# Moving the last down products of a conditioned FFN beside attention, with its mixing, zero fill, lists and loads

## The chip, the cores and the metric

The kernel runs on one core of one Trainium2 chip. The metric is the device time of one execution in microseconds, the median over several runs. The engines are written as in the profile: PE (matrix products), PEld (loading of PE's weights, which overlaps), DVE (vector), ACT (activations), POOL, SP (which here only issues transfers). ACT and POOL issue transfers too. DMA stands for the 16 transfer engines.

## The reference, cut to what matters

Everything is float32. `x` has 4 batches of 512 tokens and 256 columns; `cond` gives eight weights for each batch.

```python
def reference(x, cond, ...):
    # 1. conditioned FFN: each batch uses the expert of its largest condition
    e = argmax(cond, -1)
    c = (silu(x @ Wu[e].T + bu[e]) * (x @ Wg[e].T + bg[e])) @ Wd[e].T + bd[e]
    # 2. attention over 512 tokens: 16 query heads of 16 columns, one shared k and v
    x = x + softmax(q(c) @ k(c).T) @ v(c) @ Wo.T + bo
    # 3. a dense layer whose weights are mixed from 8 for each batch
    w = einsum('bg,got->bot', cond, weight * mask)
    t = x @ w[b].T + bias2
    # 4. top-2 routing over 8 experts, 128 places for each expert in each group
    #    of 256 tokens, then gelu(t @ wi[e]) @ wo[e], weighted and summed
    return x + moe(t)
```

## The kernel before

The tile program is written out by hand: the order in which the Python code emits the instructions is the order on each engine. Five stretches follow each other on PE.

*The conditioned FFN* (`hidden`, L268; `down`, L258). For each of four batches `b`, `hidden(b, hc)` makes a quarter of the hidden columns: products with two weights into two PSUM banks (L279, L281), Silu on ACT (L283), a product on DVE (L284) into the tile `hid`. `down(b, dc)` multiplies `hid` by the second weights, 512 tokens at a time in four accumulated products (L263), and ACT adds the bias and writes `coT` (L264). Batches 0 to 2 are emitted by the loop at L347. Beside it DVE mixes the third part's weights: `mixed(b, g)` (L244) adds expert `g`'s masked weights `w2_sb` into `wb_sb` of batch `b`; there are 32 of them, four emitted after each quarter from (1, 1) on. In batch 2's quarters the first attention's projections are emitted (L359): the queries go through DRAM (`qd`, L319 and L320) to reach the layout of the score products.

*The zero fill* (L361). ACT's queue writes zeros to `xp`, the buffer in DRAM to which tokens are scattered later; 8,712 KB in one transfer.

*The lead* (L797). Attention runs in 64 steps, 16 for each batch. Step `n` makes the exponentials for step `n` and the row maxima for step `n + LEAD`, with `LEAD = 6`. So six sets of maxima are made first (`maxima`, L366: four products of 32 rows, L375, and four reductions on DVE, L379). The list `before_steps` (L789) says what PE does between them: batch 3's hidden quarters, the down products of batches 2 and 3, and, for the third part, `turn_mixed` (L689, transposes of the mixed weights) and `route_mixed` (L700, their product with the router).

*Attention* (L1123). A step has `maxima`, `exponentials` (L396: products L405, Exp on ACT L409) and `weigh` (L414: products L423 with the exponentials of the step before). Four 32-row products use the array together, two of maxima and two of exponentials. Two forms of a step exist. The sparse one weighs in two halves; the dense one puts other PE work (`side`) between its two half sets and weighs once. A step is dense if the table `beside` (or `last`, for batch 3) names PE work at that step. Those tables also hold the later parts of the batches before: values, their normalisation (`inv`, `norm`), output product, `mix` (third part), routing (`choose`, `rank`, `places`, `rows`), and the scatter of the tokens to `xp` on POOL's queue (`send`, `row0` to `row3`; two indirect transfers each, L656).

*The FFN of the experts* (`run`, L1189). Units of 256 or 128 tokens with one expert: fetch weights (`fetch_in`, `fetch_out`: 1 MB each on SP's queue, L912) and rows (`fetch_rows`, L929, which waits for scatters so far), transpose (`turn`, L972, and the DVE copy L980), `up` (L1036, products L1051), `put` (L1077, products L1084) and an adding scatter to the output (L1098). Weight tiles have three buffers each. Which expert and which rows a unit has comes from lists that DVE works out (`list_of_pairs`, L866; `lists_of_rest`, L882). `first_pairs` emits the first ones within the last attention, `place` (L1168) and the table `final` (L761) put batch 3's remaining pieces and the list of the rest between the pieces of the first units.

SBUF is given out by pools: `cp` and `c1p` hold the first part's tiles and are closed at L805, before the attention's pools `ep`, `rp` and `fp` are opened in their place. [...]

Of the kernel before, what the change touches and what calls it, by code (L numbers as in the profile page):

```python
# [42 lines left out]
def adaln_attn_ffn_kernel(  # L43
# [77 lines left out]
    qp = attn_ctx.enter_context(tc.tile_pool(name="qp", bufs=2))  # L121
    c1 = ExitStack()
# [3 lines left out]
    w2_sb = c1p.tile([P, NE, 2 * D], F32, name="w2_sb")  # L126
# [131 lines left out]
    def down(b, dc):  # L258
        w = w_of[b][1]
        wd = w[:, 0:1024].rearrange("p (c d) -> p c d", c=4)  # L260
        po = bank("x")
        for hc in range(4):
            mm(po, wd[:, hc, ts(dc, P)], hid_of[b][:, hc, :], start=hc == 0, stop=hc == 3)  # L263
        nc.scalar.activation(  # L264
            coT[:, dc, ts(b, T)], po, AF.Identity, bias=w[:, 1032 + dc : 1033 + dc]
        )

    def hidden(b, hc):  # L268
        w, w2 = w_of[b]
        wu, wg = (  # L270
            w[:, ds(512 * hc + 256 * n, 256)].rearrange("p (c h) -> p c h", c=2)
            for n in range(2)
        )
        if hc == 0:
            hid_of[b] = cp.tile([P, 4, T], F32, name="hid")
# [71 lines left out]
    for b in range(B - 1):  # L347
        for hc in range(4):
            hidden(b, hc)
            if (b, hc) > (1, 0):  # L350
                for _ in range(4):
                    mixed(*mixing.pop(0))
# [7 lines left out]

    nc.scalar.dma_start(  # L361
        xp.rearrange("(p r) c -> p r c", p=P),
        zeros.unsqueeze(1).to_broadcast([P, NE * EROWS // P + 2, XROW]),
    )

# [334 lines left out]
    def route_mixed(b):  # L700
# [60 lines left out]
    final = {  # L761
# [8 lines left out]

    def side(b, k):

        for off, name in (last if b == B - 1 else beside)[k]:
# [14 lines left out]

    before_steps = [  # L789
        [(hidden, B - 1, 0), (down, B - 2, 0)],  # L790
        [(down, B - 2, 1), (hidden, B - 1, 1), (turn_mixed, 0), (turn_mixed, 1)],
        [(hidden, B - 1, 2), (route_mixed, 0), (route_mixed, 1), (turn_mixed, 2)],
        [(hidden, B - 1, 3), (route_mixed, 2), (turn_mixed, 3)],
        [(down, B - 1, 0), (route_mixed, 3)],
        [(down, B - 1, 1)],
    ]
    for m in range(LEAD):  # L797
        maxima(m, (0, 1, 2, 3))
        if m == 3:
            shifted(0)  # L800
        for f, *of in before_steps[m]:
            f(*of)
        while mixing:
            mixed(*mixing.pop(0))
# [3 lines left out]
    fp = attn_ctx.enter_context(tc.tile_pool(name="fp", bufs=2))  # L808
# [8 lines left out]
    pairs = fp.tile([P, NE + 1], F32, name="pairs", bufs=1)  # L817
    nc.gpsimd.memset(pairs, 0.0)
    texp = fp.tile([P, NUNIT], F32, name="texp", bufs=1)
    table = fp.tile([P, 2, NUNIT], I32, name="table", bufs=1)  # L820
    count = fp.tile([P, 1], I32, name="count", bufs=1)

# [59 lines left out]
    def lists_of_rest():  # L882
        for _ in list_of_pairs(NA, NB):
            pass
        got = fp.tile([P, NE], F32, name="got", bufs=1)
# [17 lines left out]
        nc.vector.tensor_copy(count, most)  # L903
# [43 lines left out]
    def first_pairs(part):  # L947
# [17 lines left out]
        elif part == "5":  # L965
            turn(0, "x")
        else:
            i = fetch_in(2)
            tc.add_manual_dep(i.ins, weighed[-1].ins.name, AFTER, reason="not at once")
            fetch_out(1)  # L970
# [65 lines left out]
    def up(u, half):  # L1036
# [10 lines left out]
        for f0 in range(4 * half, 4 * half + 4, each):  # L1047
            ph = bank("m")
            for k in range(each):
                for c in range(2):  # L1050
                    mm(  # L1051
                        ph[:, ts(k, n)], wi_of[u][:, c, ts(f0 + k, P)], xT_of[u][:, c, :],
                        start=c == 0, stop=c == 1,
                    )
            nc.scalar.activation(  # L1055
# [67 lines left out]
    for n in range(STEPS + 1):  # L1123
        m = n + LEAD
        if n in (0, 27, 43, 56):
# [5 lines left out]
        )  # L1131
# [36 lines left out]
    def place():  # L1168

        for name in final.get(next(places), ()):  # L1170
            if name == "rest":
                lists_of_rest()
                ready.update(range(NA, NUNIT))
                for f, u in late:
                    f(u)
                late.clear()
            else:
                work[B - 1][name]()

    ready, late = set(range(NA)), []  # L1180
# [8 lines left out]
    def run(units, rows, begun=False):  # L1189
# [3 lines left out]
        for k in range(len(units) + 1):  # L1193
            for u in units[k : k + 1]:
                for x in rows(k):
                    fetch_rows(units[x])
                if begun and k == 0:
# [6 lines left out]
                for x in units[k + 3 : k + 4]:  # L1204
                    fetch(fetch_in, x)
# [11 lines left out]
            for x in units[k + 2 : k + 3]:  # L1217
                fetch(fetch_out, x)
# [9 lines left out]
    def rows_behind(k):  # L1228
        return (k + 2,) if k + 2 < len(units) else ()
# [96 lines left out]
```

## Time and profile before

| | |
|---|---|
| median of 3 runs | 650.72 us (650.18 to 651.39) |
| profiled execution | 648.59 us, span 646.9 us |
| mean granted PE clock | 0.992 |
| conditioned FFN up to the first maxima | 0 to 68.2 us |
| lead | 68.2 to 108.8 us |
| first attention, 16 steps | 108.8 to 171.2 us |
| whole attention | 108.8 to 381.9 us |
| FFN of the experts | to 631 us, then the last scatters |

The stretches are read from the timeline of PE: the lead begins with the first product of L375, the first attention with the first of L405. The costliest groups of the page (line, engine, operation, out<-in, tile, count; busy us and mean ns; idle time before them and what ended most of it):

```profile
L379 DVE TENSOR_REDUCE negm<-ps_m 128x1 f32<-128x512 f32 x250 | 160.7, 686 | 63.1 <-PE ps_x L405 43.6
L409 ACT ACTIVATE e<-ps_x 128x512 f32<-128x512 f32 x244 | 132.5, 595 | 100.6 <-PE ps_x L405 96.9
L375 PE MATMUL ps_m<-k,q 32*128 32x512 f32 x500 | 153.3, 639 | 0.0
L405 PE MATMUL ps_x<-q,k 32*128 32x512 f32 x488 | 139.1, 639 | 0.0
L1051 PE MATMUL ps_m<-xT,wi_sb 128*128 128x256 f32 (+1 forms) x672 | 115.5, 330 | 3.2 <-issue 3.2
L1084 PE MATMUL ps_x<-wo_sb,e 128*128 128x256 f32 x512 | 114.3, 379 | 0.0
L423 PE MATMUL ps_a<-e,v 128*32 128x256 f32 (+1 forms) x792 | 75.6, 454 | 0.6 <-ACT e L409 0.2
L263 PE MATMUL ps_x<-hid,wo_sb 128*128 128x512 f32 x64 | 28.8, 597 | 0.0
```

Each product of the program counts twice here, since a float32 product is carried out in two passes. The means are longer than the distance between starts, because the passes overlap; the timeline of PE gives the distance.

### The profile page before, as it was taken

The numbers are of one execution on the slowest core, as the hardware profiler recorded it, in microseconds if no ns is written. First come the engines' busy times: TensorE is split into PE (matmuls) and PEld (weight loads), VectorE is DVE, ScalarE is ACT, GpSimd is POOL, SyncE is SP. The second block draws the span as 40 slices with busy tenths as digits, with TensorE's granted clock in tenths as the row PEclk, the third lists the DMA queues.
The fourth block names the chain that finished last, engine by engine and source line by source line (L and its number), as shares of the span: only waits on it lengthen the run. The fifth ranks groups of instructions, "written<-read, shape, count | busy, mean of one in ns | idle before, by whom it ended". The sixth has DMA issues, their size and how long they took to land.

```text
span 646.9 us, 10162 instructions
## 1 busy us (share of the span) xinstructions
PE 624.3 (97%) x3736; PEld 364.0 (56%) x3736; DVE 335.2 (52%) x831; ACT 226.2 (35%) x404; POOL 111.3 (17%) x146
## 2 busy tenths in 40 slices
PE   8999999999999999999999989999999999999990
PEld 3444454333333433343335268887899999778880
DVE  1174844677768677876887744358222221322320
ACT  1212123566655555654653742221111111111220
POOL 1600000000000000310031141225332222313332
PEclk9999999999999999999999999999999999999996
DMA  7952981300142204321033399736889999888711
GB/s 234 358 167 72 310 269 34 98 19 18 34 132 68 67 18 117 135 68 48 19 121 100 130 334 271 237 99 208 233 275 317 323 333 315 254 275 264 209 20 19
DMA packets 65403, 107.11 MB, mean 166 GB/s; under 512 B 6914, under 2 KB 26946, under 8 KB 65346
## 3 DMA queue, kind: packets, MB, share of 16 engines
q1 hardware_dynamic: 50066, 87.96, 41.8%
q0 software_dynamic: 6400, 8.72, 6.7%
q10 hardware_dynamic: 8880, 9.71, 4.8%
q8 instruction: 31, 0.51, 0.3%
q14 instruction: 26, 0.21, 0.1%
HBM read 79.59 MB, written 26.65 MB: 164 GB/s over the span
## 4 chain that ended last, share of the span: by engine, by line
PE 91%; DMA 2%; DVE 2%; issue 1%; ACT 1%; POOL 1%; SPq 0%; POOLq 0%; DVEq 0%
PE ps_m L375 20%; PE ps_m L1051 17%; PE ps_x L1084 16%; PE ps_a L423 10%; PE ps_a L279 4%; PE ps_x L263 4%; PE ps_x L281 4%; PE ps_x L535 2%; PE ps_x L313 2%; PE ps_x L503 2%; PE ps_x L405 1%; PE ps_a L978 1%; PE ps_x L328 1%; PE ps_x L1018 1%; PE ps_m L995 1%
## 5 line engine op out<-in xcount | busy, mean ns | idle before, releaser
L379 DVE TENSOR_REDUCE negm<-ps_m 128x1 f32<-128x512 f32 x250 | 160.7, 686 | 63.1 <-PE ps_x L405 43.6
L409 ACT ACTIVATE e<-ps_x 128x512 f32<-128x512 f32 x244 | 132.5, 595 | 100.6 <-PE ps_x L405 96.9
L375 PE MATMUL ps_m<-k,q 32*128 32x512 f32 x500 | 153.3, 639 | 0.0
L405 PE MATMUL ps_x<-q,k 32*128 32x512 f32 x488 | 139.1, 639 | 0.0
L1051 PE MATMUL ps_m<-xT,wi_sb 128*128 128x256 f32 (+1 forms) x672 | 115.5, 330 | 3.2 <-issue 3.2
L1084 PE MATMUL ps_x<-wo_sb,e 128*128 128x256 f32 x512 | 114.3, 379 | 0.0
L1051 PEld LDWEIGHTS ps_m<-xT,wi_sb 128*128 128x128 f32 x672 | 103.6, 191 | 13.7 <-issue 4.5
L1084 PEld LDWEIGHTS ps_x<-wo_sb,e 128*128 128x128 f32 x512 | 95.6, 190 | 12.6 <-issue 0.4
L1055 ACT ACTIVATE e<-ps_m 128x512 f32<-128x512 f32 x64 | 38.0, 597 | 173.5 <-PE ps_m L1051 165.7
L375 PEld LDWEIGHTS ps_m<-k,q 32*128 32x128 f32 x500 | 46.5, 183 | 65.7 <-DVE negm L379 36.5
L1098 POOL DMA_INDIRECT out_dram<-y,to_row x36 | 55.5, 1542 | 136.9 <-DVE at L1074 31.6
L423 PE MATMUL ps_a<-e,v 128*32 128x256 f32 (+1 forms) x792 | 75.6, 454 | 0.6 <-ACT e L409 0.2
L423 PEld LDWEIGHTS ps_a<-e,v 128*32 128x32 f32 x792 | 15.6, 108 | 74.9 <-issue 62.5
L980 DVE COPY xT<-ps_a 128x256 f32<-128x256 f32 (+1 forms) x23 | 12.1, 528 | 81.0 <-PE ps_a L978 81.0
L1094 DVE TENSOR_SCALAR y<-ps_x,w 128x256 f32<-128x256 f32 x32 | 15.3, 482 | 58.5 <-PE ps_x L1084 58.5
L656 POOL DMA_INDIRECT xp<-x,to_i x32 | 33.1, 1036 | 55.7 <-DVE negm L379 25.1
L405 PEld LDWEIGHTS ps_x<-q,k 32*128 32x128 f32 x488 | 38.1, 183 | 0.2
L585 POOL TENSOR_SCALAR x<-mk 128x4 f32<-128x4 f32 x4 | 0.8, 211 | 205.4 <-DVE mk L582 205.3
L284 DVE SCALAR_TENSOR_TENSOR hid<-ps_x,wo_sb,sg 128x512 f32<-128x512 f32 x16 | 12.0, 749 | 45.5 <-PE ps_x L281 45.5
L279 PE MATMUL ps_a<-xT_sb,wi_sb 128*128 128x512 f32 x64 | 30.5, 599 | 0.4 <-DMA wi_sb<-in_wcond_dram 0.3
L281 PE MATMUL ps_x<-xT_sb,wi_sb 128*128 128x512 f32 x64 | 30.1, 592 | 0.0
L263 PE MATMUL ps_x<-hid,wo_sb 128*128 128x512 f32 x64 | 28.8, 597 | 0.0
(166 smaller groups left out, 465.1 us busy)
## 6 DMA issues: line engine op xcount, KB each, us to landing
wi_sb<-in_wi_dram SPq DMA_DIRECT2D x25, 1024.0 KB
wo_sb<-in_wo_dram SPq DMA_DIRECT2D x25, 1024.0 KB
xp<-zeros ACTq DMA_DIRECT2D x1, 8712.0 KB
q<-qd SPq DMA_DIRECT2D x8, 512.0 KB
wi_sb<-in_wcond_dram SPq DMA_DIRECT2D x15, 256.0 KB
od<-stage SPq DMA_DIRECT2D x15, 256.0 KB
xt<-xp SPq DMA_DIRECT2D x11, 264.0 KB
wo_sb<-in_wcond_dram SPq DMA_DIRECT2D x4, 517.0 KB
```

The lines of the kernel that those rows point to most:

```text
L263: mm(po, wd[:, hc, ts(dc, P)], hid_of[b][:, hc, :], start=hc == 0, stop=hc == 3)
L279: mm(pu, wu[:, c, :], xT_sb[:, c, ts(b, T)], start=c == 0, stop=c == 1)
L281: mm(pg, wg[:, c, :], xT_sb[:, c, ts(b, T)], start=c == 0, stop=c == 1)
L375: mm(pm, q[32 * j : 32 * j + 32, i, ts(hg, P)], k[32 * j : 32 * j + 32, :], start=True, stop=True,)
L379: nc.vector.tensor_reduce(nm[:, i, j : j + 1], pm, AX.X, ALU.max, negate=True)
L405: mm(px, k[rows_j, ts(sc, P)], seqs[u // 4]["q"][rows_j, :, ts(u % 4, P)], start=True, stop=True,)
L409: nc.scalar.activation(e_of[n][:, :, j, :].rearrange("p h (i t) -> p i h t", i=4), px.rearrange("p (i h t) -> p i h t", i=4, h=4), AF.Exp,)
L423: i = mm(pa_of[u][32 * hh : 32 * hh + 32, j0 * P : (j0 + nj) * P], seqs[b]["v"][:, sc, :], e[:, hh, j0 : j0 + nj].rearrange("p j n -> p (j ...
L1051: mm(ph[:, ts(k, n)], wi_of[u][:, c, ts(f0 + k, P)], xT_of[u][:, c, :], start=c == 0, stop=c == 1,)
L1055: nc.scalar.activation(hT_of[u][:, f0 : f0 + each].rearrange("p f t -> p (f t)"), ph, AF.Gelu_apprx_tanh,)
L1084: mm(po[:, 0:D], hT_of[u][:, fc, ts(h, P)], wo_of[u][:, fc, :], start=fc == 0, stop=fc == F // P - 1,)
L1098: i = nc.gpsimd.indirect_dma_start(out=out_rows, out_offset=bass.IndirectOffsetOnAxis(ap=to, axis=0), in_=y, in_offset=None, compute_op=AL ...
```

## The change

Six things are done together.

1. Batch 3's down products leave the lead. Each is cut into two halves of 256 tokens and put into the first attention at steps 4, 6, 8 and 9. These steps become dense. The tile `hid` of batch 3 and `w2_sb` move to a pool of their own (`hp`), which is kept until step 16; the pool `fp` is opened only then.
2. Batch 3's eight mixings (`mixed`) leave the FFN loop and the lead, two to each of those four steps. The turns and routes of batches 2 and 3 leave the lead for steps 12 and 13, which become dense as well. Within the lead the order is new: hidden quarters with the first two turns and routes first, batch 2's down products last.
3. The zero fill is issued before batch 2's hidden quarters, not after them.
4. In the last attention, `values`, `inv` and `norm0` of the batch before come one step earlier.
5. `row1` of batch 2 moves one step later, `row2` and `row3` behind the last attention step. Of batch 3, `row1` to `row3` are spread over two more places. The loads of units 2 and 3 (`fetch_in`, `fetch_out`) are emitted behind the fetching of their rows.
6. The list of the rest is made in four pieces (pairs, singles, halves, quarters), at four places instead of one.

On PE nothing is added or left out: the two down products are 16 products of 256 columns instead of 8 of 512, and six steps weigh once instead of in two halves.

```diff
+    c2 = ExitStack()
+    hp = c2.enter_context(tc.tile_pool(name="hp", bufs=1, side="right"))
...
-    w2_sb = c1p.tile([P, NE, 2 * D], F32, name="w2_sb")
+    w2_sb = hp.tile([P, NE, 2 * D], F32, name="w2_sb")
...
-    def down(b, dc):
+    def down(b, dc, half=None):
+        n = T if half is None else T // 2
+        t0 = 0 if half is None else half * n
...
-        po = bank("x")
+        po = bank("x")[:, 0:n]
         for hc in range(4):
-            mm(po, wd[:, hc, ts(dc, P)], hid_of[b][:, hc, :], start=hc == 0, stop=hc == 3)
+            mm(
+                po, wd[:, hc, ts(dc, P)], hid_of[b][:, hc, ds(t0, n)], start=hc == 0,
+                stop=hc == 3,
+            )
...
     for b in range(B - 1):
+        if b == B - 2:
+            nc.scalar.dma_start(
+                xp.rearrange("(p r) c -> p r c", p=P),
+                zeros.unsqueeze(1).to_broadcast([P, NE * EROWS // P + 2, XROW]),
+            )
         for hc in range(4):
             hidden(b, hc)
             if (b, hc) > (1, 0):
                 for _ in range(4):
-                    mixed(*mixing.pop(0))
+                    if len(mixing) > NE:
+                        mixed(*mixing.pop(0))
...
-    nc.scalar.dma_start(
-        xp.rearrange("(p r) c -> p r c", p=P),
-        zeros.unsqueeze(1).to_broadcast([P, NE * EROWS // P + 2, XROW]),
-    )
...
     last = [
         [(-2, "rank0")],
-        [(-2, "rank1")],
-        [(-1, "values"), (-2, "places"), (-2, "rows")],
-        [(-1, "inv"), (-2, "send")],
-        [(-2, "row0")],
-        [(-1, "norm0"), (-1, "norm1"), (-2, "row1")],
+        [(-1, "values"), (-2, "rank1")],
+        [(-2, "places"), (-2, "rows"), (-1, "inv")],
+        [(-2, "send")],
+        [(-1, "norm0"), (-2, "row0")],
+        [(-1, "norm1"), (-2, "row1")],
...
-        [(0, "pairs4"), (-1, "row1"), (-1, "row2")],
-        [(0, "pairs5"), (-1, "row3")],
-        [(0, "bias"), (0, "pairs6")],
+        [(0, "pairs4")],
+        [(0, "pairs5"), (-1, "row1")],
+        [(0, "bias")],
     ]
...
     final = {
-        0: ["inv0"], 2: ["values1"], 4: ["inv1", "norm0", "norm1"],
+        0: ["-row2", "-row3", "inv0"], 2: ["values1"], 4: ["inv1", "norm0", "norm1"],
...
-        11: ["places", "rows", "send", "row0", "row1", "row2", "row3"], 12: ["rest"],
+        11: ["places", "rows", "send", "row0"], 12: ["row1", "rest"], 13: ["row2", "row3", "rest"],
+        14: ["rest"], 15: ["rest"],
     }
...
+    halves = {
+        k: [(down, B - 1, dc, half)]
+        for k, (dc, half) in zip((4, 6, 8, 9), itertools.product(range(2), range(2)))
+    }
+    halves[12] = [(turn_mixed, 2), (turn_mixed, 3)]
+    halves[13] = [(route_mixed, 2), (route_mixed, 3)]
+
     def side(b, k):
 
+        for f, *of in halves.get(k, ()) if b == 0 else ():
+            f(*of)
+            if f is down:
+                mixed(*mixing.pop(0))
+                mixed(*mixing.pop(0))
...
     before_steps = [
-        [(hidden, B - 1, 0), (down, B - 2, 0)],
-        [(down, B - 2, 1), (hidden, B - 1, 1), (turn_mixed, 0), (turn_mixed, 1)],
-        [(hidden, B - 1, 2), (route_mixed, 0), (route_mixed, 1), (turn_mixed, 2)],
-        [(hidden, B - 1, 3), (route_mixed, 2), (turn_mixed, 3)],
-        [(down, B - 1, 0), (route_mixed, 3)],
-        [(down, B - 1, 1)],
+        [(hidden, B - 1, 0), (turn_mixed, 0), (turn_mixed, 1)],
+        [(hidden, B - 1, 1), (route_mixed, 0)],
+        [(hidden, B - 1, 2), (route_mixed, 1)],
+        [(hidden, B - 1, 3)], [(down, B - 2, 0)], [(down, B - 2, 1)],
     ]
...
-    fp = attn_ctx.enter_context(tc.tile_pool(name="fp", bufs=2))
...
     def lists_of_rest():
         for _ in list_of_pairs(NA, NB):
             pass
+        yield range(NA, NA + NB)
...
-        nc.vector.tensor_copy(count, most)
+            if u0 == UQUARTER:
+                nc.vector.tensor_copy(count, most)
+            yield range(u0, u0 + n)
...
+        if n == 16:
+            c2.close()
+            fp = attn_ctx.enter_context(tc.tile_pool(name="fp", bufs=2, side="right"))
...
-        )
+        ) or (b == 0 and k in halves)
...
             if name == "rest":
-                lists_of_rest()
-                ready.update(range(NA, NUNIT))
+                ready.update(next(rest))
                 for f, u in late:
-                    f(u)
-                late.clear()
+                    if u in ready:
+                        f(u)
+                late[:] = [(f, u) for f, u in late if u not in ready]
+            elif name[0] == "-":
+                work[B - 2][name[1:]]()
...
+                if begun and k == 1:
+                    for n in (2, 3):
+                        fetch_in(units[n])
+                        fetch_out(units[n - 1])
...
     def rows_behind(k):
-        return (k + 2,) if k + 2 < len(units) else ()
+        first = {0: (), 1: (2, 3)}
+        return first.get(k, (k + 2,) if k + 2 < len(units) else ())
```

More of the change, by code (lines that the diff above doesn't have):

```diff
@@ L256, in adaln_attn_ffn_kernel @@
     hid_of = {}
-    def down(b, dc):
+    def down(b, dc, half=None):
+        n = T if half is None else T // 2
+        t0 = 0 if half is None else half * n
         w = w_of[b][1]
         wd = w[:, 0:1024].rearrange("p (c d) -> p c d", c=4)
-        po = bank("x")
+        po = bank("x")[:, 0:n]
         for hc in range(4):
-            mm(po, wd[:, hc, ts(dc, P)], hid_of[b][:, hc, :], start=hc == 0, stop=hc == 3)
+            mm(
+                po, wd[:, hc, ts(dc, P)], hid_of[b][:, hc, ds(t0, n)], start=hc == 0,
+                stop=hc == 3,
+            )
         nc.scalar.activation(
-            coT[:, dc, ts(b, T)], po, AF.Identity, bias=w[:, 1032 + dc : 1033 + dc]
+            coT[:, dc, ds(b * T + t0, n)], po, AF.Identity, bias=w[:, 1032 + dc : 1033 + dc]
         )
@@ L274, in hidden @@
         if hc == 0:
-            hid_of[b] = cp.tile([P, 4, T], F32, name="hid")
+            hid_of[b] = (
+                cp.tile([P, 4, T], F32, name="hid") if b < B - 1
+                else hp.tile([P, 4, T], F32, name=f"hid{b}")
+            )
         pu = bank("a")
@@ L347, in adaln_attn_ffn_kernel @@
     for b in range(B - 1):
+        if b == B - 2:
+            nc.scalar.dma_start(
+                xp.rearrange("(p r) c -> p r c", p=P),
+                zeros.unsqueeze(1).to_broadcast([P, NE * EROWS // P + 2, XROW]),
+            )
         for hc in range(4):
@@ L802, in adaln_attn_ffn_kernel @@
             f(*of)
-        while mixing:
-            mixed(*mixing.pop(0))
     c1.close()
@@ L816, in adaln_attn_ffn_kernel @@
     NUNIT = UQUARTER + NE
[L817 to L821, printed above, removed]
     def of_experts(t, less, op, begin):
@@ L964, in first_pairs @@
             fetch_out(0)
-        elif part == "5":
+        else:
             turn(0, "x")
[L967 to L970, printed above, removed]
     def turn(u, tag="a"):
@@ L1050, in up @@
                 for c in range(2):
-                    mm(
+                    i = mm(
                         ph[:, ts(k, n)], wi_of[u][:, c, ts(f0 + k, P)], xT_of[u][:, c, :],
@@ L1054, in up @@
                     )
+            if u == 0:
+                weighed.append(i)
             nc.scalar.activation(
@@ L1124, in adaln_attn_ffn_kernel @@
         m = n + LEAD
+        if n == 16:
+            c2.close()
+            fp = attn_ctx.enter_context(tc.tile_pool(name="fp", bufs=2, side="right"))
+            pairs = fp.tile([P, NE + 1], F32, name="pairs", bufs=1)
+            nc.gpsimd.memset(pairs, 0.0)
+            texp = fp.tile([P, NUNIT], F32, name="texp", bufs=1)
+            table = fp.tile([P, 2, NUNIT], I32, name="table", bufs=1)
+            count = fp.tile([P, 1], I32, name="count", bufs=1)
         if n in (0, 27, 43, 56):
@@ L1171, in place @@
             if name == "rest":
-                lists_of_rest()
-                ready.update(range(NA, NUNIT))
+                ready.update(next(rest))
                 for f, u in late:
-                    f(u)
-                late.clear()
+                    if u in ready:
[3 more added lines that the diff above has]
+                work[B - 2][name[1:]]()
             else:
                 work[B - 1][name]()
+    rest = lists_of_rest()
     ready, late = set(range(NA)), []
@@ L1204, in run @@
                 for x in units[k + 3 : k + 4]:
-                    fetch(fetch_in, x)
+                    if not begun or k > 0:
+                        fetch(fetch_in, x)
                 for x in units[k + 1 : k + 2]:
@@ L1217, in run @@
             for x in units[k + 2 : k + 3]:
-                fetch(fetch_out, x)
+                if not begun or k > 0:
+                    fetch(fetch_out, x)
     singles = range(NA + NB, NA + NB + NTILE)
```

## The prediction

> **What bounds the kernel.** I read the page first: busy shares and the chain of waits.
>
> ```profile
> PE 624.3 (97%) x3736; PEld 364.0 (56%) x3736; DVE 335.2 (52%) x831; ACT 226.2 (35%) x404; POOL 111.3 (17%) x146
> ...
> PE 91%; DMA 2%; DVE 2%; issue 1%; ACT 1%; POOL 1%; SPq 0%; POOLq 0%; DVEq 0%
> ```
>
> PE is busy from 7 to 631 us and is 91% of the chain that ended last. So the end moves only if PE has less to do, or waits less, and "busy" may hide waits. I therefore read PE's timeline next, step by step, in the first attention (two sparse half steps) and in the third (a dense step):
>
> ```profile
> 133.85 0.64 PE L423 MATMUL ps_a<-e,v 128*32 128x256 f32 x8
> ...
> 135.71 0.64 PE L423 MATMUL ps_a<-e,v 128*32 128x256 f32 x8
> ...
> 137.39 0.64 PE L423 MATMUL ps_a<-e,v 128*32 128x256 f32 x8
> ...
> 277.70 1.99 PE L503 MATMUL ps_x<-wo_sb,attn 128*128 128x256 f32 x8
> 279.63 0.70 PE L375 MATMUL ps_m<-k,q 32*128 32x512 f32 x2
> ...
> 280.70 1.06 PE L423 MATMUL ps_a<-e,v 128*32 128x512 f32 x8
> ...
> 282.77 1.56 PE L503 MATMUL ps_x<-wo_sb,attn 128*128 128x256 f32 x6
> ```
>
> A sparse step (maxima, exponentials, weighing, nothing beside) takes 137.39 - 133.85 = 3.54 us. A dense step takes 282.77 - 277.70 = 5.07 with 1.93 (277.70 to 279.63) of other products in it, so 3.14 for the same attention work: a sparse step holds about 0.4 us of waiting (for the reductions that free the PSUM banks) that the row "busy" covers. Then the lead, the six steps of maxima before the first attention:
>
> ```profile
> 99.70 3.70 PE L263 MATMUL ps_x<-hid,wo_sb 128*128 128x512 f32 x8
> 103.24 0.95 PE L706 MATMUL ps_x<-wr_sb,stage 128*128 128x8 f32 x8
> 104.12 0.71 PE L375 MATMUL ps_m<-k,q 32*128 32x512 f32 x3
> ...
> 105.19 3.70 PE L263 MATMUL ps_x<-hid,wo_sb 128*128 128x512 f32 x8
> 108.83 0.70 PE L375 MATMUL ps_m<-k,q 32*128 32x512 f32 x2
> ```
>
> Here every piece follows the one before without a gap: a down product of 512 columns 3.54 (the last 3.64), a route 0.88, a set of maxima 1.07. Nothing is hidden in the lead; what leaves it saves its full length. Last, three waits that the timelines of DVE and PE show late in the run:
>
> ```profile
> 338.13 1.85 DVE L486 TENSOR_TENSOR attn<-o,inv 128x512 f32<-128x512 f32 x2
> 339.26 4.07 PE L503 MATMUL ps_x<-wo_sb,attn 128*128 128x256 f32 x16 [0.81 <-issue]
> ...
> 376.52 0.69 DVE L980 COPY xT<-ps_x 128x512 f32<-128x512 f32 x1 [3.04 <-PE ps_a L423]
> 377.26 3.72 PE L1051 MATMUL ps_m<-xT,wi_sb 128*128 128x256 f32 x16 [2.06 <-issue]
> ...
> 451.73 0.68 DVE L980 COPY xT<-ps_a 128x512 f32<-128x512 f32 x1
> 452.51 7.14 PE L1051 MATMUL ps_m<-xT,wi_sb 128*128 128x256 f32 x32 [1.15 <-issue]
> ```
>
> PE waits 0.81 us for the normalisation, 2.06 us (375.20 to 377.26, in the chain) for the first xT copy, and 1.15 us for a later xT copy that stands behind 16 us of list arithmetic on DVE.
>
> [...] 97% busy, yet 3.54 against 3.14 us for the same work. [...] The trace gives a set of eight 32-row passes in 1.07 us against 0.43 us for one full pass (3.44/8): 3.2 times. So attention's products fill the array, and a full product put beside them adds its own length. [...] No moment of this trace shows a long ACT transfer beside SP's, so that cost is open.
>
> **The change, part by part.**
>
> 1. *Out of the lead.* Both down products of batch 3 (3.54 + 3.64), two turns (0.57 + 0.56), two routes (0.81 + 0.88): 10.0, of which 0.1 is the tail of whatever comes last. **-9.9.** The down products of batch 2 only move within it.
>
> 2. *Into the first attention.* Four steps (4, 6, 8, 9) get half a down product: eight passes of 256 columns, half of 3.54 = 1.77, so 3.14 + 1.77 = 4.91, +1.37 each, +5.5 together. DVE has four reductions (2 x 1.29) and two mixings (3.10 for four at 63.44, so 0.78 each): 4.14, under 4.91; without that cover a step would be as long as DVE's work and its gaps, some 5.3. Short side work gains less: the step with rT and v took 4.96 (216.38 to 221.34) for 1.02 + 0.53, so 3.41 beside. Step 12, two turns (0.96): 4.37, +0.83. Step 13, two routes (1.69): 4.83 to 5.10, taken as 4.97, +1.43. Together **+7.8**. Parts 1 and 2: -2.1. DVE's eight mixings leave the time 68 to 78, where PE did not wait for them: nothing.
>
> 3. *Zero rows sooner.* The queue of ACT, the transfers of q on SP:
>
> ```profile
> 59.98 1.08 SPq L319 DMA_DIRECT2D qd<-stage  x2
> 62.91 0.33 SPq L320 DMA_DIRECT2D q<-qd  x1
> 66.27 0.68 ACTq L361 DMA_DIRECT2D xp<-zeros  x1
> ...
> 68.00:70.00 2.00, 2.00 (x13) 0.81 (x12) 1.93 (x4) 0.00 (x0) 0.00 (x0) 1.00 1.04 356
> ...
> 92.00:94.00 2.00, 2.00 (x16) 1.07 (x16) 0.37 (x2) 0.59 (x1) 0.00 (x0) 1.00 0.87 270
> ```
>
> The fill takes 67.6 to 93.6, 26 us at some 342 GB/s, with the engines full (share 1.04 to 1.09). It now issues behind the last hidden activation of batch 1, at 43.9; with the same 1.3 us to its first byte it would run 45.2 to 71.2, alone. Now the q transfers (0.26 MB written, 0.52 read, twice) fall into it: +0.9 MB/342 = 2.7, to 73.9. In the built order the last write of q's second half waits for the fill's completion [...]. From 73.9: write 2.4 (62.91 less the second issue, 60.52), read 3.1 (62.91 to 66.0): lands 79.4. PE needs it at the third set of maxima: 68.18 + 2 x (1.07 + 3.54) + 0.96 + 0.81 + 0.45 = 79.6. Queued behind the waiting SP: the nmT transfers, due only near 90. Bounds 0 and +6.5 (rival A); I take **+0.5**, as the two times meet.
>
> 4. *Last attention.* Values, inv and norm0 one step earlier. norm0 (0.93) falls into DVE's idle 0.94 at 333.8; its input lands near 333.3 (iv at 327.3, 1.4 to the write, 4.0 for inv, as at 197.84). Then PE starts at 338.45, waits about 0.2 for norm1 and ends at 342.1, not 343.25: **-1.1** (0 to -1.4).
>
> 5. *Scatters and loads at the turn to the FFN.* The 2.06 us: DVE and ACT both stand still from 373.5 to 376.5, while eight scatters and two 1 MB loads run. Four of the eight scatters now come after the last weighing, and two later loads move behind. Bounds -2.06 and 0; no row settles it: **-1.0**. New: the rows of unit 2 wait for those four scatters. Counted from the last weighing's end (381.9): scatters 4 x 1.29 = 5.2, landed +2 to +5 (444.6 to 449.67 beside loads), rows land +2.5: 9.7 to 12.7, while PE turns unit 2 at +11.0; then wi of unit 2, behind them, lands at 16 to 19, needed at +18.4. **+0.4** (0 to +1.7).
>
> 6. *Lists in four pieces.* The xT copy now stands before the fourth list (3.6 us, 447.9 to 451.5), so it is done near 448.8, before PE comes at 451.37: **-1.15**. The fourth list is wanted only 100 us later. The last two scatter pairs move behind two adds on POOL and end some 2 us later; unit 6's rows (issued 449.67, used 459.5) have 5 us to spare. Pool and table moves: nothing.
>
> Sum: -9.9 + 7.8 + 0.5 - 1.1 - 1.0 + 0.4 - 1.15 = **-4.45** (-4.5). The profiled execution took 648.59 us (span 646.9 and 1.7 around it): 644.1. The median of the runs shown is 650.72, 2.13 above the profiled one; the same gain gives **646.3**.
>
> **Rivals.** *A, the fill starves q (slower).* Place: the first maxima, due at 68.18. If SP's transfers of q advance only when the fill is through (71.2, then read 3.1 and overhead), PE starts near 74.7: 6.5 instead of 0.5, so 650.72 + 1.5 = 652.3. It decides for slower once q's first half lands later than about 74.5; q alone took 54.83 to 61.0 and so may double without cost. For it: engines full, and an ACT transfer of 256 KB that took 391.35 to 402.1 beside SP loads. Against: q's rows are longer pieces than the fill's, and there are 7 us of slack. *B, the side work gives nothing.* DVE's 4.14 plus gaps bounds the four steps (5.3, +1.6), and unit 2's rows come late (+1.3 more): 649.2. For: DVE is in one line with the banks; against: dense steps of 5.07 show no such wait. *C, the stall at 375 stays whatever is queued*: 647.4, inside the forecast's range.
>
> **How the numbers follow.** Forecast with C 0.62 (own range 644.5 to 648.5), B 0.18, A 0.12; 0.08 for what I don't see, on both sides. A measurement of this kernel tells about 0.2% (1.3 us) from no change. B splits 0.10 faster, 0.08 same: faster 0.62 + 0.10 + 0.04 = 0.76, slower 0.12 + 0.02 = 0.14, same 0.10. Range: best ends of parts 3 to 5 (-0.5, -0.3, -1.06, -0.4) give 644.0, a little room 643.6; above, B and half of the way to A: 650.8.
>
> **What would show it.** The lead should end near 99 to 100 instead of 108.83, with a gap at the first or third maxima if A works; the six steps should take 4.9 (5.0 for routes, 4.4 for turns); PE's wait of 0.81 and that of 1.15 gone; the turn of unit 2 without a gap. Wrong if the steps with a down half are over 5.3, or PE stands for q over 5 us, or a new wait shows at units 1 to 3.

## The result, and the profile after

The changed kernel takes 647.68 us (median of 20 executions, 645.0 to 651.1), the kernel before 650.45 beside it (20 executions, 648.15 to 652.58). The ratio is 0.9957, 95% interval 0.9943 to 0.9971: a gain of 2.8 us (1.9 to 3.7) where 4.45 was forecast. The profiled executions lie nearer to each other (648.39 us with a span of 646.6, against 648.59 and 646.9), because the one of the changed kernel holds a stretch of half clock (mean 0.987) and that of the kernel before none (0.992). Why single executions of one kernel differ by 2 us is itself a finding, and comes up below.

The page's shares and chain of the changed kernel look much the same as before, except for two entries of the chain: DMA is now 5% of it, not 2%, and PE 89%, not 91%.

```profile
PE 625.3 (97%) x3704; PEld 366.0 (57%) x3704; DVE 334.5 (52%) x831; ACT 226.3 (35%) x406; POOL 110.9 (17%) x146
...
PE 89%; DMA 5%; issue 1%; POOL 1%; DVE 1%; ACT 1%; SPq 0%; POOLq 0%; DVEq 0%
```

The chain of waits between 60 and 75 us shows the first piece of it (start, length, what):

```profile
55.08 7.90 DMA qd<-stage
62.98 0.02 SPq L332
63.00 0.03 issue
63.03 7.36 DMA q<-qd
70.39 0.04 issue
70.44 1.23 PE ps_m L388 x3
```

The first half of `q` now takes 15.3 us from the start of its write to the end of its read (55.08 to 70.39). In the kernel before, the same write and read went like this on SP's queue, and the data was there at 60.9:

```profile
54.83 1.11 SPq L319 DMA_DIRECT2D qd<-stage  x2
57.75 0.34 SPq L320 DMA_DIRECT2D q<-qd  x1
```

PE, ready at 67.98, stands 2.46 us in front of the first maxima. The cause stands on ACT's queue: the zero fill was issued at 40.17 us, 3.7 us earlier than the forecast had it, and filled the transfer engines until about 70.5 (DMA share 0.99 from 67.98 to 70.44).

```profile
40.17 0.68 ACTq L362 DMA_DIRECT2D xp<-zeros  x1
```

The stretches of the changed kernel (span, busy us of PE, PEld, DVE, ACT and POOL, granted PE clock, DMA share, GB/s) show what followed that wait:

```profile
70.00:72.00 2.00, 1.56 (x8) 0.52 (x8) 0.00 (x0) 0.00 (x0) 0.00 (x0) 0.60 0.30 99
72.00:74.00 2.00, 2.00 (x6) 0.84 (x3) 1.46 (x3) 0.00 (x0) 0.00 (x0) 0.54 0.07 18
74.00:76.00 2.00, 2.00 (x6) 0.95 (x5) 1.03 (x2) 0.69 (x1) 0.00 (x0) 1.00 0.26 51
```

PE works, but at half its clock: taken half a microsecond at a time, it reads 0.50 from 70.5 to 73.5 and 0.67 in the half microsecond behind. The same work (from the first maxima to the first exponentials) took 32.7 us here, and 31.1 us in kernels without that stretch. So the lead ends at 103.17, not at the 99 to 100 of the forecast:

```profile
99.53 3.70 PE L268 MATMUL ps_x<-hid,wo_sb 128*128 128x512 f32 x8
103.16 0.70 PE L388 MATMUL ps_m<-k,q 32*128 32x512 f32 x2
103.17 0.70 PE L418 MATMUL ps_x<-q,k 32*128 32x512 f32 x2
...
119.22 0.64 PE L436 MATMUL ps_a<-e,v 128*32 128x256 f32 x8
121.11 0.64 PE L436 MATMUL ps_a<-e,v 128*32 128x256 f32 x8
122.96 1.99 PE L268 MATMUL ps_x<-hid,wo_sb 128*128 128x256 f32 x8
125.96 1.06 PE L436 MATMUL ps_a<-e,v 128*32 128x512 f32 x8
128.03 0.64 PE L436 MATMUL ps_a<-e,v 128*32 128x256 f32 x8
129.93 0.64 PE L436 MATMUL ps_a<-e,v 128*32 128x256 f32 x8
```

The last six of these lines are steps of the first attention. A step with a half of a down product goes from 121.11 to 125.96: 4.85 us. The sparse step behind it goes from 125.96 to 129.93: 3.97, not 3.54. The first attention as a whole (first query product to the next batch's) takes 70.83 us, against 62.40.

Late in the run the three waits of the kernel before read as follows, again on PE's timeline:

```profile
338.80 0.64 PE L436 MATMUL ps_a<-e,v 128*32 128x256 f32 x8
340.44 4.08 PE L516 MATMUL ps_x<-wo_sb,attn 128*128 128x256 f32 x16
...
346.37 1.07 PE L436 MATMUL ps_a<-e,v 128*32 128x512 f32 x8
...
376.20 1.06 PE L436 MATMUL ps_a<-e,v 128*32 128x512 f32 x8
377.20 3.72 PE L1068 MATMUL ps_m<-xT,wi_sb 128*128 128x256 f32 x16
...
401.26 3.69 PE L1068 MATMUL ps_m<-xT,wi_sb 128*128 128x256 f32 x16 [1.05 <-DMA wi_sb<-in_wi_dram]
...
445.52 7.07 PE L1103 MATMUL ps_x<-wo_sb,e 128*128 128x256 f32 x32
452.43 7.07 PE L1068 MATMUL ps_m<-xT,wi_sb 128*128 128x256 f32 x32
```

The stall of 2.06 us before unit 0's up products is gone (377.20 follows the weighing), and so is that of 1.15 near 452. A new one of 1.05 us stands at 401.26, for the input weights of unit 2. The wait for the normalisation is gone from in front of the output products at 340, but from the weighing before these products to the one behind them (338.80 to 346.37) it is still 7.57 us, as against 7.76 in the kernel before.

### The profile page after: what moved, and what is told of

It reads as the page before. It is cut to its first block, busy times and chain, and to the rows that moved or that the text cites. A ratio compares the mean times of both kernels' runs of the same rounds, so it can differ in the third digit from the quotient of the medians.

```text
span 646.6 us, 10096 instructions
## 1 busy us (share of the span) xinstructions
PE 625.3 (97%) x3704; PEld 366.0 (57%) x3704; DVE 334.5 (52%) x831; ACT 226.3 (35%) x406; POOL 110.9 (17%) x146
## 4 chain that ended last, share of the span: by engine, by line
PE 89%; DMA 5%; issue 1%; POOL 1%; DVE 1%; ACT 1%; SPq 0%; POOLq 0%; DVEq 0%
PE ps_m L388 22%; PE ps_m L1068 15%; PE ps_x L1103 15%; PE ps_a L436 10%; PE ps_x L268 4%; PE ps_a L291 4%; PE ps_x L293 3%; PE ps_x L548 2%; PE ps_x L516 2%; PE ps_x L325 2%; DMA wi_sb<-in_wi_dram 2%; PE ps_x L418 1%; DMA qd<-stage 1%; DMA q<-qd 1%; PE ps_a L995 1%
## 5 line engine op out<-in xcount | busy, mean ns | idle before, releaser
L1068 PEld LDWEIGHTS ps_m<-xT,wi_sb 128*128 128x128 f32 x672 | 103.6, 191 | 11.5 <-issue 2.3
L436 PEld LDWEIGHTS ps_a<-e,v 128*32 128x32 f32 x744 | 14.6, 108 | 70.3 <-issue 60.3
L1113 DVE TENSOR_SCALAR y<-ps_x,w 128x256 f32<-128x256 f32 x32 | 15.3, 482 | 58.9 <-PE ps_x L1103 58.9
L268 PE MATMUL ps_x<-hid,wo_sb 128*128 128x512 f32 (+1 forms) x80 | 29.4, 515 | 0.0
L295 ACT ACTIVATE sg<-ps_a,wo_sb 128x512 f32<-128x512 f32 x16 | 11.0, 687 | 51.4 <-PE ps_a L291 43.8
```

Source lines behind the costliest of these rows:

```text
L268: mm(po, wd[:, hc, ts(dc, P)], hid_of[b][:, hc, ds(t0, n)], start=hc == 0, stop=hc == 3,)
L436: i = mm(pa_of[u][32 * hh : 32 * hh + 32, j0 * P : (j0 + nj) * P], seqs[b]["v"][:, sc, :], e[:, hh, j0 : j0 + nj].rearrange("p j n -> p (j ...
L1068: i = mm(ph[:, ts(k, n)], wi_of[u][:, c, ts(f0 + k, P)], xT_of[u][:, c, :], start=c == 0, stop=c == 1,)
```

## The experiments

There are twelve runs, in three groups. The kernel before was timed in each group, and takes another time in each: 650.11, 646.07 and 649.95 us (the last two on the same chip). So ratios are to the kernel before of the same group.

| label | what it is | us | ratio (95%) |
|---|---|---|---|
| e1_fill_back | changed kernel, fill at its old place | 643.85 | 0.9901 (0.9884 to 0.9919) |
| e2_fill_alone | kernel before, fill sooner | 653.42 | 1.0056 (1.0038 to 1.0074) |
| e3_wi_first | changed, unit 2's weights ahead of its rows | 652.87 | 1.0040 (1.0025 to 1.0055) |
| e4_list_whole | changed, list in one stretch | 655.13 | 1.0077 (1.0056 to 1.0098) |
| e5_wo_later | e1, output weights of unit 1 later | 643.32 | 0.9965 (0.9953 to 0.9978) |
| e6_loads_back | e1, two loads as before | 650.07 | 1.0056 (1.0043 to 1.0069) |
| e7_scatters_back | e1, scatters as before | 642.89 | 0.9948 (0.9936 to 0.9961) |
| e9_parts12 | parts 1 and 2 alone | 643.78 | 0.9964 (0.9951 to 0.9978) |
| e11_before | kernel before, a profile | 648.77 | |
| e13_parts12 | as e9 | 647.81 | 0.9962 (0.9946 to 0.9977) |
| e12_fill_back | as e1 | 644.02 | 0.9911 (0.9886 to 0.9936) |
| e10_best | e1 with three edits | 643.32 | 0.9895 (0.9873 to 0.9917) |

The first four rows are the first group, the next four the second, the last four the third. One of e2's twelve executions took 2,146 us; the ratio leaves it out.

**The zero fill, taken back and alone.** Both directions, one edit each. This is e1, in the changed kernel; e2 is the reverse, in the kernel before:

```diff
-        if b == B - 2:
-            nc.scalar.dma_start(
-                xp.rearrange("(p r) c -> p r c", p=P),
-                zeros.unsqueeze(1).to_broadcast([P, NE * EROWS // P + 2, XROW]),
-            )
         for hc in range(4):
             hidden(b, hc)
...
+    nc.scalar.dma_start(
+        xp.rearrange("(p r) c -> p r c", p=P),
+        zeros.unsqueeze(1).to_broadcast([P, NE * EROWS // P + 2, XROW]),
+    )
     def maxima(m, js):
```

> The changed kernel with the zero fill issued again behind the last hidden activation of batch 2, nothing else touched. Theory T (the early fill slows q's transfers, PE stands 2.5 us before the first maxima and then runs at a low granted clock for about 4 us, 1.6 us more): q's first half lands near 66, the first maxima start near 68.0 without a wait, the granted clock stays at 1.00 between 70 and 76, and the time falls by 4.1 us, to about 643.6 (ratio to the kernel before near 0.9895). Rival U (the drop in the clock has nothing to do with the wait and comes with the new order of the lead): the wait goes, the low clock between 70 and 76 stays, gain 2.5 us, to about 645.2. Rival V (the fill, running until about 93 again, now holds up the transfers of the negated maxima that the first exponentials need about 6 us sooner than in the kernel before): a wait of 2 to 5 us appears at the first exponentials near 97, and the time stays at 646 to 648.

> The kernel before with the zero fill alone issued sooner, in front of batch 2's hidden products. Theory T: a wait of about 2.5 us before the first maxima, the granted clock near 0.55 to 0.6 for the 4 us behind it, and a time about 4.1 us over the kernel before (ratio near 1.006). Rival U: the wait of 2.5 us without the low clock, ratio near 1.004. Rival W (q's transfers wait in the changed kernel for another reason than the fill): no wait, ratio 1.000.

PE's timeline of e1:

```profile
67.97 0.60 PE L347 MATMUL ps_x<-ident,k 128*128 128x128 f32 x4
68.50 0.71 PE L387 MATMUL ps_m<-k,q 32*128 32x512 f32 x3
...
69.57 1.99 PE L291 MATMUL ps_a<-xT_sb,wi_sb 128*128 128x512 f32 x4
```

Theory T holds in e1: no wait, a clock of 1.00 from 70 to 76, and the first exponentials at 99.62. The fill (issued at 66.59) leaves no wait at those exponentials either, so V falls, and U with the full clock. In e2 the same wait comes with the fill alone:

```profile
70.36 1.23 PE L377 MATMUL ps_m<-k,q 32*128 32x512 f32 x3 [2.29 <-DMA q<-qd]
...
380.34 5.41 PE L1053 MATMUL ps_m<-xT,wi_sb 128*128 128x256 f32 x16 [2.09 <-DVE xT L982]
```

It costs 0.0056 of 650, 3.6 us (2.5 to 4.8), and taking it back gives the same from the other side (0.9957 less 0.9901). T's 4.1 lies within that; by their mean clock (0.991 and 0.992 in two of e2's executions) not all of them have the stretch of half clock.

The second line shows something that nobody had expected. The 2 us stall that the kernel before has near 375 is there too, and the 16 products behind it take 5.41 us instead of 3.72. The stretches of e2 at that place say why:

```profile
378.00:380.00 2.00, 0.26 (x4) 0.00 (x0) 0.40 (x1) 0.30 (x1) 1.68 (x2) 1.00 0.99 313
380.00:382.00 2.00, 1.66 (x5) 1.39 (x6) 1.42 (x2) 1.15 (x3) 1.71 (x1) 0.71 0.99 349
382.00:384.00 2.00, 2.00 (x6) 1.55 (x6) 0.00 (x0) 0.83 (x2) 1.39 (x3) 0.50 1.04 411
```

In the profiled kernel before, the same stall (2.06 us) left the clock at 1.00 from 374 to 384. So a stall of 2 us cost 2.06 us in one execution and 2.09 + (5.41 - 3.72) = 3.8 in another; what decides between the two no run shows.

**Unit 2's weights ahead of its rows.**

```diff
+                if begun and k == 1:
+                    i = fetch_in(units[2])
+                    tc.add_manual_dep(i.ins, weighed[-2].ins.name, AFTER, reason="not at once")
                 for x in rows(k):
                     fetch_rows(units[x])
                 if begun and k == 1:
-                    for n in (2, 3):
-                        fetch_in(units[n])
-                        fetch_out(units[n - 1])
+                    fetch_out(units[1])
+                    fetch_in(units[3])
+                    fetch_out(units[2])
```

> The changed kernel with unit 2's input weights issued ahead of the rows of units 2 and 3 on SP's queue, after unit 0's first half of up products. Theory: these weights are late (PE stands 1.1 us near 400) only because they queue behind rows that wait for the four late scatters; issued near 382 they land near 393, the wait goes, and the time falls by 1.0 us, to about 646.7 (ratio near 0.9941). Rival: the rows now come later beside the 1 MB of weights, and PE stands for them instead, or a load beside the scatters costs as much elsewhere: no gain, ratio near 0.9957.

The theory fell, and it fell by 5 us. PE's timeline of e3:

```profile
397.29 1.11 PE L995 MATMUL ps_a<-ident,xt 128*128 128x128 f32 x4 [4.74 <-DMA xt<-xp]
398.20 9.15 PE L1103 MATMUL ps_x<-wo_sb,e 128*128 128x256 f32 x32
```

The rival is right: the rows are now the late ones. Issued at 390.68 (388.75 in the changed kernel, where PE used them at 392.70 without a wait), they came at 397.3, beside 1 MB of weights. The wait of 4.74 us brought the low clock back: the 32 products behind it took 9.15 us instead of 7.07 (mean clock 0.984 in this profile, 0.987 in the changed kernel's). The new wait of 1.05 at 401 is the smaller evil of the two.

**The list in one stretch.**

```diff
-        11: ["places", "rows", "send", "row0"], 12: ["row1", "rest"], 13: ["row2", "row3", "rest"],
-        14: ["rest"], 15: ["rest"],
+        11: ["places", "rows", "send", "row0"], 12: ["row1", "rest", "rest", "rest", "rest"],
+        13: ["row2", "row3"],
```

> The changed kernel with the four lists of the rest again built in one stretch on VectorE. If the split is what took away the stall of 1.15 us near 452, it comes back: time 1.15 us over the changed kernel (648.8, ratio near 0.9975) and an idle of about 1.1 us before the up products near 452. Rival: with loads and scatters placed as in the changed kernel the copy of the transposed rows is in time anyway: ratio near 0.9957.

Neither was right. The stall near 452 did not come back, as the rival has it; but the kernel is 0.0120 (7.8 us) slower than the changed one. POOL's timeline and PE's:

```profile
451.92 1.58 POOL L1117 DMA_INDIRECT out_dram<-y,to_row  x1 [9.38 <-DVE xT L997]
453.80 1.01 POOL L669 DMA_INDIRECT xp<-x,to_i  x1 [0.30 <-issue]
```

```profile
463.82 0.69 PE L995 MATMUL ps_a<-ident,xt 128*128 128x128 f32 x2 [4.76 <-DMA xt<-xp]
464.30 8.88 PE L1103 MATMUL ps_x<-wo_sb,e 128*128 128x256 f32 x32
```

An add to the output stands on POOL for 9.38 us behind DVE's list arithmetic, and the last four scatters stand behind that add, since the change put them there. They are issued from 453.80 on, where the changed kernel has them at 445.13; the first rows of the rest wait for all of them and are issued at 460.88 instead of 455.71. So splitting the list and moving the scatters belong together. The forecast had priced them as two edits.

**The wait at 401, and the stall at 375.** Three kernels on the base of e1. First e5, unit 1's output weights and the loads behind them after unit 1's up products (two helper lines are left out here):

```diff
                 if begun and k == 1:
-                    for n in (2, 3):
-                        fetch_in(units[n])
-                        fetch_out(units[n - 1])
+                    fetch_in(units[2])
...
                 up(u, 1)
+                if begun and k == 1:
+                    i = fetch_out(units[1])
+                    tc.add_manual_dep(i.ins, weighed[-1].ins.name, AFTER, reason="not at once")
+                    fetch_in(units[3])
+                    fetch_out(units[2])
```

e6, unit 2's input and unit 1's output weights in the last attention step (they leave `run`):

```diff
-        [(0, "bias")],
+        [(0, "bias"), (0, "pairs6")],
...
-        else:
+        elif part == "5":
             turn(0, "x")
+        else:
+            i = fetch_in(2)
+            tc.add_manual_dep(i.ins, weighed[-1].ins.name, AFTER, reason="not at once")
+            fetch_out(1)
```

e7, all scatters in the last attention steps:

```diff
-        [(0, "pairs4")],
-        [(0, "pairs5"), (-1, "row1")],
+        [(0, "pairs4"), (-1, "row1"), (-1, "row2")],
+        [(0, "pairs5"), (-1, "row3")],
...
-        0: ["-row2", "-row3", "inv0"], 2: ["values1"], 4: ["inv1", "norm0", "norm1"],
+        0: ["inv0"], 2: ["values1"], 4: ["inv1", "norm0", "norm1"],
```

> The kernel of e1 (changed kernel, fill at its old place), in which the output weights of unit 1 and all loads behind them are issued only after unit 1's up products, so that unit 2's input weights have the transfer engines to themselves for their first 2 us. Theory: these 1 MB took 10 us (391.1 to 401.1 in the changed kernel) because they shared with 1 MB of output weights; alone they take 3 to 6 us, the wait of 1.2 us near 397 goes and the time falls by 1.2, to about 642.6 (ratio near 0.9882). Rival: the output weights of unit 1 or the input weights of unit 3 are now the late ones, a wait of 1 us or more shows at 409 or 419, and the time stays at 643.9 or goes above.

> The kernel of e1 with the loads of unit 2's input and unit 1's output weights back in the last attention step, the four scatters left late. If these 2 MB are what makes VectorE and ScalarE stand for 3 us at 373 to 376 in the kernel before, the stall of 2 us before unit 0's up products is back, and the wait of 1.2 us near 397 is gone: +0.8, so 644.7, and 646.4 in executions in which the stall also halves the granted clock for 3.4 us. If the eight scatters in a row are what does it (or both together are needed), no stall, and without the wait near 397 the time is 642.6 (ratio near 0.9882).

> The kernel of e1 with all eight scatters of the two last row blocks again in the last attention steps, the loads left late. If the scatters make the stall at 373 to 376, it is back (2 us), while the rows of unit 2 and so its weights come some 6 us sooner and the wait near 397 goes: 644.7 to 646.4. If the loads make it, or both are needed: no stall, no wait near 397, 642.6 (ratio near 0.9882).

The expected ratios took the kernel before at 650; in this group it took 646.07, so they can't be compared. What can be read are the waits of the profiles, and the kernels of the group beside each other. In e5 the wait for unit 2's weights is 0.73 us (1.24 in e1's profile, 0.80 in e12's): little of what was expected. In e7 it is 0.95: counted from unit 0's up products, the last scatter is issued 3.8 us sooner than in e1 (5.1 against 8.9 us), but the rows only 1.1 us (10.4 against 11.5). In e6 the weights are early and the rows late once more:

```profile
394.05 1.12 PE L998 MATMUL ps_a<-ident,xt 128*128 128x128 f32 x4 [6.01 <-DMA xt<-xp]
```

With the 2 MB queued at 372, the rows could be issued only at 386.91, 5.7 us after the last of the late scatters (2.7 in e5), and took 7.1 us to come. So late scatters and early loads do not go together; the change had to move both. On the stall at 375 these two runs say nothing, because in this group not even e9 has it, which keeps all of the old order there. So no run tells which of the two moves, scatters or loads, takes it away.

**Parts 1 and 2 alone, and the kernel before again.** e9 and e13 are one kernel: e1 with `last`, `final`, the scatters, the loads and the list as in the kernel before.

> Only parts 1 and 2 of the change: the down products, turns and routes of the last batch beside the first attention, with the pools this needs; fill, last attention, scatters, loads and lists as in the kernel before. The sum of the forecast is -9.9 + 7.8 = -2.1, so a ratio near 0.9968; the profiled changed kernel's own steps (lead ends 9.8 sooner without the wait, first attention 8.4 longer) say -1.4 (0.9978). Rival: the steps beside the down halves cost as much as they save in the lead, ratio 1.000.

> Parts 1 and 2 of the change alone, a second time, for its profile and time beside the kernel before on one chip. It has the scatters and loads at the turn to the FFN as in the kernel before. If the stall near 375 belongs to them, it has the stall whenever the kernel before has it, and the ratio is 0.9968 to 0.9978 (gain 1.4 to 2.1). If parts 1 and 2 themselves take it away (by moving the turn in time), there is none here while the kernel before has it: ratio 0.994 or less (gain 4 or more, with the half clock behind it).

> The kernel before, unaltered, for its profile beside the other runs of this call (the times of the kernel before differ between calls: 650.1 us in the first, 646.1 in the second). Theory H: its executions near 648.5 have the stall of 2 us near 375 and a full clock, those near 650.5 to 651 have the same stall and in addition one stretch of 3.41 us of half clock behind it (mean clock lower by 0.0026, 1.7 us), and those near 646 have no stall there at all. Rival: the stall of 2 us is there in all of them and the difference of 4 us lies elsewhere, for instance in longer transfers.

The gain is 0.0036 of 646.07 = 2.3 us and 0.0038 of 649.95 = 2.5. The stall at 375 differs with the group, not with parts 1 and 2: none in e9, 2.10 us in e13, and 0.63 in e11, which is the kernel before. The one near 452 does the same: none in e9, 1.42 in e13, 1.07 in e11. Theory H of e11 was thus too neat: e11 is an execution of 648.77 with the full clock, but with a third of the stall. What does hold is the arithmetic of the clock. In the third group's 20 executions of the kernel before, the ten with a mean clock of 0.991 or more took 648.39 to 649.64 us, and nine of the ten with less took 650.38 to 652.87 at 0.986 to 0.989. One stretch of 3.41 us at half clock (its length in the changed kernel's profile, 70.42 to 73.83) lowers the mean over 647 us by 3.41 x 0.5 / 647 = 0.0026, and costs up to 1.7 us.

The profile of e9 has such a stretch in a place with no stall at all, step 13 of the first attention (PE's timeline, then stretches as above):

```profile
159.20 1.95 PE L718 MATMUL ps_x<-wr_sb,stage 128*128 128x8 f32 x16
161.08 1.14 PE L387 MATMUL ps_m<-k,q 32*128 32x512 f32 x2
```

```profile
158.00:160.00 2.00, 2.00 (x19) 1.11 (x16) 1.06 (x3) 1.44 (x4) 0.00 (x0) 1.00 0.15 55
160.00:162.00 2.00, 2.00 (x15) 1.51 (x18) 0.83 (x3) 0.46 (x1) 0.00 (x0) 0.80 0.20 76
162.00:164.00 2.00, 2.00 (x16) 0.20 (x8) 0.90 (x2) 0.82 (x2) 0.00 (x0) 0.50 0.00 0
164.00:166.00 2.00, 2.00 (x20) 0.45 (x16) 0.75 (x3) 0.27 (x1) 0.00 (x0) 0.85 0.05 13
```

It follows the two routes, 16 passes with only 8 columns each. The eight weighing products of this step took 1.83 us in e9. The profiles of e7 and e13 have the same (1.89 and 1.82 us); in e1 and e12, with the same routes ahead, they took 1.06.

**Three edits on e1.** e12 is e1 again, for comparison.

```diff
-    halves[13] = [(route_mixed, 2), (route_mixed, 3)]
+    halves[13] = [(route_mixed, 2)]
+    halves[14] = [(route_mixed, 3)]
...
 # as e5, and the rows of unit 3 behind unit 2's input weights
+                    fetch_in(units[2])
+                    fetch_rows(units[3])
```

> The kernel of e1 a second time (changed kernel, fill at its old place), as the reference for the two others on this chip. 643.3 to 644.2 in the first call; with the waits that its profile shows (none before 397) it depends on the chip little: 643 to 644.5.

> The kernel of e1 with unit 1's output weights issued behind its up products (as in e5), the rows of unit 3 issued behind the input weights of unit 2, and the two routes of one attention step put into two steps. Theory: the wait of 1.2 us for unit 2's input weights (0.7 in e5) is gone; two routes in a row (1.95 us of passes of 8 columns) no longer bring the stretch of half clock that the profiles with a lower mean clock show at 162 us: 642.0 to 642.8, 1 to 1.5 us under e1 on the same chip, with no execution over 645. Rival: two steps with one route each cost more than one with two (a step with any side work takes 3.96 instead of 3.54): no gain over e5's 643.3.

e10 gives 643.32 where 642.0 to 642.8 was expected, e12 644.02; the intervals overlap, so no gain is proved. Steps 13 and 14 take 4.12 and 4.13 us, against 5.02 and 3.96 in e12, but the next dense step gives 0.4 back. The wait for unit 2's weights is still 1.10 us. None of e10's six executions is over 643.98 (mean clock 0.990 or 0.991); one of e12's six took 646.32 at 0.988, and one execution is no proof. Both beat the kernel before by 6 to 7 us, and the changed kernel by 3 to 4.

## Why the prediction came out as it did

*Part 1, lead: -9.9.* From the first maxima to the first exponentials the kernel before takes 40.66 us (both profiles), e1 and e12 31.12: -9.5. Right.

*Part 2, first attention: +7.8.* Measured +8.4. The half steps were priced well: 4.85, 4.63, 4.85 and 5.06 us against 4.91. Step 12 takes 4.11 (forecast 4.37), step 13 5.02 (4.97). (In the step with rT and v that the turns were priced from, the transposes of rT took 0.93 us, 216.38 to 217.31, and not 1.02; that is 0.1 us.) What was left out are the steps between: a sparse step behind a dense one takes 3.96 us, not 3.54, and the sparse steps together are 1.3 us longer. Unforeseen in the other direction, the second attention is 0.3 to 1.2 us shorter than in the three profiles that have the old first attention, where DVE waits 0.21 to 1.20 us for the normalisation's transfer. Parts 1 and 2 as a whole: -2.1 forecast, -2.3 and -2.5 measured. Rival B, the side work that gives nothing, is out.

*Part 3, zero fill: +0.5.* Measured +3.6. This is the step that failed, and it failed in the way of rival A. The term that failed is the cost of q's transfers beside the fill. It was taken as their bytes over the full rate (0.9 MB / 342 GB/s = 2.7 us, all on the fill's end), as if SP's transfers went on undisturbed. The packets of the changed kernel's trace show otherwise. Once a transfer moved (packets of 2,048 and 4,096 bytes beside the fill's of 1,056), it took longer than alone: the read of q's first half (0.52 MB) moved in 3.0 us beside the fill, 175 of some 342 GB/s (2.2 us alone), and its write (0.26 MB) in 3.6 us (1.4 alone). The larger part went before that. The first packet moved 4.2 us after the issue of the write and 3.9 after that of the read, where the kernel before has 1.1 and 1.0; e2, e3 and e4 have 3.9 to 4.2 as well. Why a first packet waits so long no run shows. As the read needs the write, the chain of two paid it twice: q's first half came at 70.4 where 68.0 was needed. The forecast had worried about the second half, put at 79.4 and there at 78.2, in time (SP's last write of it waited 8.1 us for the fill). A second term was misread, but did little: the fill was put at 43.9, behind ACT's activation at 43.82, which is batch 2's first; batch 1's last is the one at 40.38. At 43.9 it would have lain over q's first half as well. Then came the half clock, which the forecast did not have at all. A's own size (6.5) was too high, as it let nothing through until the fill's end.

*Part 4, last attention: -1.1.* In the changed kernel's profile nothing came of it. The output products follow the weighing 1.64 us behind its start, not 2.70, so the wait is gone; but the set of maxima and exponentials behind them takes 1.92 us, not 1.07, as DVE stands 2.26 us for the output products and begins the four additions only at 344.50, and the steps ahead are 0.2 us longer. From the first query products of the last batch to its last, the five profiles with the old order take 60.5 to 60.6 us; the changed kernel takes 60.6, e1, e3, e4, e10 and e12 60.2 to 60.3, and e5 to e7 59.7. The scatters that moved are in this too. So it is worth 0 to 0.9, inside the bounds given (0 to -1.4), and less than the value taken.

*Part 5, turn to the FFN: -1.0 and +0.4.* Outside the second group, where nothing has it, the stall of 2.06 is absent in the six profiles with scatters and loads at or near the places where the change put them (changed kernel, e1, e3, e4, e10, e12), and present in the four with the old order (2.06, 2.09, 2.10, and 0.63 in e11). That fits a removal, and speaks against rival C. But what makes DVE and ACT stand still for 3 us in those was not settled, nor why the second group is free of it. The new wait came, and at the place named: 1.05 us (0.73 to 1.24 in the e1 family) against 0.4. It is one of the forecast's own signs of being wrong, a new wait at units 1 to 3.

*Part 6, list: -1.15.* The wait of 1.15 is gone, as reckoned. That it could only be bought together with the moved scatters was not seen.

*The sum.* In the first and third groups parts 4 to 6 come to -3.4 to -4.0 (0.9901 and 0.9911 of e1 and e12, less 2.4 for parts 1 and 2) against -2.85; a stall that is gone can also take its half clock with it (1.7 us in e2). In the second group they come to almost nothing: e5, with all of the change but the early fill (and its loads later), has 0.9965, and e9, with parts 1 and 2 alone, 0.9964 (e7 has 0.9948, and the intervals overlap). e9 shows neither of the two stalls there. So most of what these parts bring is the removal of stalls that the kernel before does not always have. With the values of the first and third groups, -2.4, +3.6 and -3.7 give -2.5, and -2.8 was measured. The forecast was right in direction on its main ground, parts 1 and 2. That it came near in size is luck: one part was priced 3 us too low, and parts whose size was a guess made up for some of it.

## What to carry to other kernels

A long transfer on one queue is not free for a short one on another: price it by how long the short one takes beside it, for each link of a chain anew, and look at whose completion is due first. Here 0.26 MB of q written beside 8.7 MB of zeros, and then read, came 2.46 us late in spite of 7 us of slack. Where scatters, the rows that wait for them, loads and list work share queues, move them as one edit and time the whole: e3, e4 and e6 altered single pieces, and each cost 5 to 8 us. A stall of PE of about 2 us should be priced as itself plus up to 1.7 us (2.09 and 1.69 in e2, 2.06 and nothing in the kernel before), and a stall seen in one profile should be looked for in a second before its removal is counted as a gain.

## What was not expected of the hardware

The half clock came as a stretch of about 3.4 us: from 70.42 to 73.83 in the changed kernel's profile (3.41 us at 0.50), and in e9's 0.80 + 2.00 + 0.60 = 3.4 us, by the means of 0.80, 0.50 and 0.85 between 160 and 166.

Near 2.1 us the length of a wait does not tell whether one follows. Behind waits of PE of 2.46 us (changed kernel), 2.29 and 2.09 (e2), 4.74 (e3) and 6.01 (e6) the low clock came. In e2 the three products of the first maxima took 1.23 us instead of 0.71, and the 16 products at 380 took 5.41 instead of 3.72; in e3 and e6 32 products took 9.15 and 9.43 us instead of 7.07. Behind 2.06 us in the kernel before the clock stayed at 1.00, and behind 2.10 us in e13 the 16 products took 3.72 us as at full clock. Nor does the work ahead of it tell: the two routes of step 13 (16 passes of 8 columns, 1.95 us in all of these profiles) had the stretch behind them without any wait in e7, e9 and e13, and not in e1, e12 and the changed kernel.

So two microseconds of waiting can be enough on this kernel, and are not always. What decides was not shown: no run moves one such wait in time and leaves everything else.
